# First attention group of a fused cross-attention and FFN kernel: source's order on SyncE and TensorE, bulk loads placed behind the turned probabilities, and a different number of value steps passed to the next group

## The chip, the cores and the metric

One core of a Trainium2 chip runs the whole program. The metric is device time in microseconds (us), the median over repeated runs; smaller is better. A core has five engines with queues of their own: TensorE (PE in the profile) multiplies matrices, VectorE (DVE) and ScalarE (ACT) work elementwise and move results out of PE's accumulators (PSUM), GpSimd (POOL) works elementwise on SBUF, and SyncE (SP) here only issues DMA transfers. Each engine takes its instructions in the order in which the built program lists them, and an instruction that has to wait holds up all behind it on that engine.

## The reference

Everything is float32. Eight sequences of 128 tokens, width 512, 32 heads of size 128, and an FFN of inner width 1376.

```python
def _L0_xattn_ref(hidden_states, key_value_states, attention_mask, position_bias, ln_weight, w_q, w_k, w_v, w_out):
    x = _rmsnorm(hidden_states, ln_weight)
    h_q = (x @ w_q.T).reshape(b, lq, H, DH)
    h_k = (key_value_states @ w_k.T).reshape(b, lk, H, DH)
    h_v = (key_value_states @ w_v.T).reshape(b, lk, H, DH)
    score = jnp.einsum('bqhd,bkhd->bhqk', h_q, h_k)
    score = score + position_bias[None]
    score = jnp.where(m, score, -jnp.inf)
    score = jax.nn.softmax(score, axis=-1)
    score = jnp.where(m, score, 0.0)
    attn = jnp.einsum('bhqk,bkhd->bqhd', score, h_v).reshape(b, lq, H * DH)
    return hidden_states + attn @ w_out.T
...
x = x + _L0_xattn_ref(_layernorm(x, axis=-1), ctx_4096, mask_BxSxS2_bk0, ...)
x = x + _L0_ffn_ref(_layernorm(x, axis=-1), ...)
```

## The kernel before

The 32 heads are worked on in eight groups of four (g = 0 to 7), and within a group the eight sequences are eight blocks (b = 0 to 7). The program runs through these stages: keys and values of group 0 (k0, v0); queries of all groups, stored to DRAM (`queries`) and loaded back two blocks at a time; the attention of group 0 to 7; the output projection; the FFN. The matrix products are split by Strassen's scheme: seven products of quarters in place of eight, and most of those seven are split once more (the inner products). So there are many sums of weight quarters on GpSimd and many additions of partial products on VectorE.

One block of attention (`probabilities`, L547) takes four score matmuls (sc, one for each head) into one PSUM bank, an addition of the masked bias s (`masked_bias`, L538, computed on GpSimd) and a maximum on VectorE, four exponentials and a sum on ScalarE, a reciprocal on VectorE and four scalings on ScalarE. Then the probabilities are turned (`transpose_p`, L582, by `turn`, L267): VectorE transposes 32x32 blocks into tt, SyncE stores tt to DRAM (`turned`, four buffers in rotation) and loads it back as pT. The product with the values (`attend`, L596: av, four matmuls, then a copy aT on ScalarE and a store) follows three blocks later: block b's turning is put on a list, and `advance(3)` (L1088) takes the one of block b - 3.

Between the blocks TensorE computes the keys and values of the next groups, as a generator of steps, `later_kv` (L644): for each group its keys and then its values. Group 1's keys are seven full products (`seven`, L336). All the others up to group 6 are two full products (`whole`, mm_k or mm_v), one single inner product (m, on two banks that alternate, seven pieces), and two pairs of inner products that run in steps of 16 short matmuls (i_k, i_v; `inner`, L382). A step's result goes out of its bank by a copy on ScalarE (into the k or v tile) or an addition on VectorE, and the bank is free for the next only then. `due` (L992) says how many units of this fill are to be done when block b of group g is finished; a full product counts 4 units (FULL), a step of an inner pair 4 (PART), a piece of the single one 1 (ONE). `late` (L996) is what each group leaves undone of its values, for the next group's blocks to fill.

Order of the work: the kernel is written against a framework that puts the instructions of each engine in an order of its own, by priorities and a timing estimate. An engine handle that is wrapped in `InOrder` (L52) keeps what is issued through it in the order of the source. At the start of group 0 `tensor`, `kv_tensor`, `vector`, `scalar` and `gpsimd` are so wrapped (L1039 to L1043). L1102 takes `tensor`, `vector` and `scalar` back to the framework's order after block 3, L1104 `kv_tensor` after block 7. DMA issues on SyncE in the attention (the bias `load_bias` L811, the weights `load_kv` L131, the queries `load_queries` L816, and the turning) are in the framework's order. A transfer into a tile also waits until the tile that held its buffer before has been read for the last time.

Of the kernel before, what the change touches and what calls it, by code (L numbers as in the profile page):

```python
# [18 lines left out]
BS = 32  # L19
# [45 lines left out]
def xattn_ffn_kernel(  # L65
# [19 lines left out]
    nc = tc.nc  # L85
# [5 lines left out]
    GH = 4  # L91
# [34 lines left out]
    def load_w(name, src, eng=nc.sync):  # L126
        t = wpool.tile([P, DC, GW], F32, tag="w", name=name)
        eng.dma_start(t, src.rearrange("(c p) n -> p c n", p=P))
        return t

    def load_kv(g):  # L131
        cols = bass.ts(g, GW)
        return load_w(f"wk{g}", wkT[:, cols]), load_w(f"wv{g}", wvT[:, cols])

    def load_q(g):
        return load_w(f"wq{g}", wqT[:, bass.ts(g, GW)], sync)
# [24 lines left out]
    kv_w = {0: (wk0, wv0)}  # L161
    x_in = [acts.tile([P, 2, D], F32, tag="a", name=f"x_{i}") for i in range(B // 2)]
    for b in range(B):
        nc.sync.dma_start(x_in[b // 2][:, b % 2, :], x[b])

    vector, gpsimd, scalar, sync = (
        InOrder(tc, e) for e in (nc.vector, nc.gpsimd, nc.scalar, nc.sync)
    )
# [410 lines left out]
        return s  # L579


    def transpose_p(g, b, p):  # L582
        n = f"{g}_{b}"
        pT = work.tile([P, 4, GH, BS], F32, tag="pT", name=f"pT_{n}", bufs=4)
        turn(
            vector, nc.sync, n, p.rearrange("q h (j r) -> q h j r", r=BS), (pT, slice(None))
        )()
        return pT

# [18 lines left out]
    tensor = kv_tensor = nc.tensor  # L608
    pend = []
# [32 lines left out]
    FULL, PART, ONE, FIRST = 4, 4, 1, 3.8  # L642
# [83 lines left out]
    kv_tensor = InOrder(tc, nc.tensor)  # L726
# [46 lines left out]
    for n, _ in enumerate(first_kv()):  # L773
        if n in moments_at:
            pair[moments_at[n]] = norm1_moments(moments_at[n])
        if n in scales_at:
            b = scales_at[n]
# [6 lines left out]
        if n in turns_at:  # L784
            b = turns_at[n]
# [18 lines left out]
    scalar = nc.scalar  # L804
# [3 lines left out]
    vector.tensor_scalar(rs1, mv1[:, :, 1], 1.0, EPS, ALU.mult, ALU.add)  # L808
    InOrder(tc, nc.scalar).activation(rs1, rs1, AF.Sqrt)

    def load_bias(g):  # L811
        pb = work.tile([P, GH, S], F32, tag="pb", name=f"pb{g}")
        nc.sync.dma_start(pb, pbias[g * GH : (g + 1) * GH].rearrange("h q k -> q h k"))
        return pb

    def load_queries(g, i, eng=nc.sync):  # L816
        q = acts.tile([P, GH, 2 * S], F32, tag="a", name=f"q_{g}_{i}")
        eng.dma_start(q, queries[g][:, :, bass.ts(i, 2 * S)])
        return q
# [5 lines left out]
    v = kvs[0][1]  # L825
# [12 lines left out]
    for g in range(NG):  # L838
# [13 lines left out]
        w, heads, name = rows_now, [], f"q{g}"  # L852
# [44 lines left out]
    biases, ahead = {0: load_bias(0)}, {}  # L897
# [8 lines left out]
    gpsimd, vector, kv_tensor = nc.gpsimd, nc.vector, nc.tensor  # L906
# [85 lines left out]
    def due(g, b):  # L992


        tiles, steps = 2 * (4 * FULL + 7 * ONE), 2 * 7 * PART
        late = 5 * PART  # L996
        if g == 0 and b < 4:
            return (5 + 2.5 * b) * FIRST
        if g < NG - 2:
            start = 12.5 * FIRST if g == 0 else g * (tiles + steps) - late  # L1000
            end, n, k = (g + 1) * (tiles + steps) - late, 4 if g == 0 else B, b - 4 if g == 0 else b
        else:
            start, n, k = g * (tiles + steps) - late, B, b
            end = start + late + 25 * FULL
        return start + (end - start) * (k + 1) / n - 1.5

    todo = [(g, i) for g in range(NG) for i in range(B // 2)]
    for g in range(NG):
        kT, v = kvs.pop(g)
        pb = biases.pop(g)  # L1010
        if g + 1 < NG:
            biases[g + 1] = load_bias(g + 1)
        if g + 2 < NG:
            kv_w[g + 2] = load_kv(g + 2)
        if g == 0:

            ctx_later = Later()
            products = later_kv()
        if g == NG - 2:
            wo_later = Later()  # L1020
            load_wo(2)(wo_later)
        if g == NG - 1:
            tensor, vector = InOrder(tc, nc.tensor), InOrder(tc, nc.vector)
            fetched, next_fetched = {}, {}
            gpsimd, sync, wo_sums = InOrder(tc, nc.gpsimd), InOrder(tc, nc.sync), None
            biased = [masked_bias(gpsimd, g, k, pb) for k in range(2)]

            bulk = InOrder(tc, nc.scalar)
            come[1, 0] = load_att(1, 0, bulk)
        for b in range(B):  # L1030
            if (g, b) == (NG - 2, B - 1):
                come = {(0, 0): load_att(0, 0, nc.sync)}
            if b % 2 == 0:
                qT = ahead.pop((g, b // 2))
                at = todo.index((g, b // 2)) + 2
                if at < len(todo):
                    ahead[todo[at]] = load_queries(*todo[at], nc.sync if g + 1 < NG else bulk)

            if (g, b) == (0, 0):  # L1039
                tensor = kv_tensor = InOrder(tc, nc.tensor)  # L1040
                vector, scalar, gpsimd = (
                    InOrder(tc, e) for e in (nc.vector, nc.scalar, nc.gpsimd)
                )  # L1043
                done = next(products) + next(products)
            if g == NG - 1:


                if b + 2 < B:
                    biased.append(masked_bias(gpsimd, g, b + 2, pb))
                for _ in range(2):  # L1050
                    wo_later.next(gpsimd)
                if wo_sums:
                    wo_sums = wo_sums(gpsimd)

                def between():
                    if b == 0:
                        next(products)
                    fetched[b] = att_sums(b, 0, come.pop((b, 0)), vector)

                p = probabilities(g, b, qT, kT, pb, between, biased.pop(0))  # L1060
            elif g == 0 and b < 4:
                def one():
                    nonlocal done
                    done += next(products)

                def one_and_sum():
                    ctx_later.next(vector)
                    one()

                if b == 0:  # L1070
                    biased = [masked_bias(gpsimd, g, k, pb) for k in range(2)]
                biased.append(masked_bias(gpsimd, g, b + 2, pb))
                p = probabilities(g, b, qT, kT, pb, one_and_sum, biased.pop(0), one)
            elif g == 0 and b < 6:
                def three_sums():
                    for _ in range(3):
                        ctx_later.next(vector)

                p = probabilities(g, b, qT, kT, pb, three_sums, biased.pop(0))
            else:  # L1080
                p = probabilities(g, b, qT, kT, pb)
                for _ in range(2):
                    ctx_later.next(vector)
                if g == NG - 2:
                    for _ in range((0, 1, 1, 1, 1, 2, 2, 2)[b]):
                        wo_later.next(InOrder(tc, nc.gpsimd))
            pend.append((g, b, transpose_p(g, b, p), v))
            advance(3)  # L1088

            if g == NG - 1:  # L1090
                while next(products, None):
                    pass
            else:
                while done < due(g, b):
                    done += next(products)
            if (g, b) == (NG - 2, 2):

                sums.close()
                wos = pools(outp)("wosA", 2, side="right", reuse_waits="tile")
                load_wo(0)(wo_later)  # L1100
                load_wo(1)(wo_later)
            if (g, b) == (0, 3):  # L1102
                tensor, vector, scalar = nc.tensor, nc.vector, nc.scalar
            if (g, b) == (0, B - 1):  # L1104
                kv_tensor = nc.tensor
            if (g, b) == (1, B - 1):
                gpsimd = nc.gpsimd
            if g == NG - 1:
                if b == 0:
                    proj.close()  # L1110
                    wos = pools(outp)("wosB", 2, reuse_waits="tile")

                    first_banks = [
                        pl.tile([P, 2, HW], F32, tag=tag, name=f"m{k}_0")
                        for k, (pl, tag) in enumerate(2 * [(ps_mm, "mm")] + 2 * [(ps_b, "i")])
                    ]
                    first_out = out_products(0, list(range(NG)), first_banks, fetched)
                n = (b + 2) % B, (b + 2) // B
                come[n] = load_att(*n, bulk)
                if b < NG - 3:  # L1120
                    wo_sums = load_wo(b + 3)
                if b:
                    next(first_out)
                if b + 2 >= B:
                    next_fetched[n[0]] = att_sums(*n, come.pop(n), gpsimd)


    scalar = InOrder(tc, nc.scalar)
# [15 lines left out]
    vector, gpsimd = nc.vector, nc.gpsimd  # L1144
# [78 lines left out]
    scalar = nc.scalar  # L1223
    for i in range(1, B // 2):
# [10 lines left out]
        tensor = nc.tensor  # L1235
# [105 lines left out]
    vector, t3 = InOrder(tc, nc.vector), h2[0, 1]  # L1341
# [227 lines left out]
    for b in range(HB):  # L1569
# [5 lines left out]
        sa, vector = coming[0], nc.vector  # L1575
# [43 lines left out]
```

## Time and profile before

| what | value |
|---|---|
| median of 3 runs | 1056.53 us (1056.42 to 1056.57) |
| the profiled execution, its own time | 1060.24 us |
| its span, first to last instruction | 1058.4 us |
| queries of all groups end, group 0's attention begins | about 227 us |
| score matmuls of group 0, blocks 0 to 7 | 230.7, 237.0, 243.1, 247.4, 254.6, 260.8, 266.0, 270.0 us |
| av matmuls of group 0, blocks 0 to 4 | 251.7, 256.4, 261.7, 266.9, 274.3 us |
| a block of scores or an av, start to start | 0.89 us |
| a full fill product, start to start | 1.73 us |
| mean granted TensorE clock | 0.998 |

The page of the profile gives the busy time of each engine, the chain of work that ended last, and the costliest groups of instructions. Other views list who waited for whom, the instructions of one engine in order of time, and the busy time in chosen windows. In a timeline line the columns are start, duration, engine, source line, operation, output and inputs, shapes and count; in square brackets stands idle time before it and what ended that. L60 is the line of the `InOrder` helper, so all wrapped instructions carry it. Names of tiles are shown without their numbers.

### The profile page before, as it was taken

To read this page: it belongs to the slowest core of one execution; us is meant where nothing else is said; L and a number is where in the kernel's file an instruction comes from. 1 tells how busy PE (TensorE), PEld (TensorE's weight loads), DVE (VectorE), ACT (ScalarE), POOL (GpSimd) and SP (SyncE) were. 2 spreads that over 40 slices of the span, in tenths; PEclk is the share of its full clock that TensorE was granted. 3 is DMA by queue.
4 is the path that set the end of the run, shared out by engine and by line. 5 is a ranking of instruction groups with operands and counts; after the bars stand their busy time and mean duration, and the time that the engine had idled before them with its cause. 6 is when DMAs were issued, how large, how long until landed. Compare 5 with 4: busy or idle time off the path is not lost.

```text
span 1058.4 us, 15313 instructions
## 1 busy us (share of the span) xinstructions
PE 1048.6 (99%) x5288; PEld 859.0 (81%) x5288; DVE 723.0 (68%) x1407; ACT 380.7 (36%) x1146; POOL 558.6 (53%) x647
## 2 busy tenths in 40 slices
PE   9999999999899999999999999999999999999998
PEld 5658888876789898988889779998888865667887
DVE  4698888885577777777777645664544247889852
ACT  2541112027555656556555555531000012333100
POOL 6649776808657666656662275570000336997010
PEclk9999999999999999999999999999999999999999
DMA  8443453495555654655656567773442622120011
GB/s 283 149 170 139 155 184 120 147 359 194 176 177 179 191 184 157 208 179 182 199 170 206 179 217 233 237 277 120 164 139 67 196 99 60 41 60 0 1 40 41
DMA packets 125854, 166.11 MB, mean 157 GB/s; under 512 B 15728, under 2 KB 77424, under 8 KB 125776
## 3 DMA queue, kind: packets, MB, share of 16 engines
q1 hardware_dynamic: 111360, 133.92, 38.5%
q10 hardware_dynamic: 12544, 24.38, 6.6%
q0 software_dynamic: 1872, 6.82, 2.1%
q8 instruction: 42, 0.69, 0.3%
q14 instruction: 36, 0.29, 0.1%
HBM read 106.90 MB, written 58.20 MB: 156 GB/s over the span
## 4 chain that ended last, share of the span: by engine, by line
PE 93%; DMA 3%; POOL 2%; DVE 1%; ACT 1%; issue 1%; SPq 0%; ACTq 0%; DVEq 0%; POOLq 0%
PE i_q L60 9%; PE m L967 9%; PE m L60 8%; PE i_v L437 7%; PE d L1525 6%; PE i L1390 6%; PE i_k L404 6%; PE mm_v L522 6%; PE mm_k L501 6%; PE mm_f L1430 5%; PE mm_q L60 4%; PE av L600 4%; PE sc L555 4%; PE mm_k L60 2%; PE mm_v L60 2%; PE m_v L437 2%
## 5 line engine op out<-in xcount | busy, mean ns | idle before, releaser
L60 DVE TENSOR_TENSOR q<-q,i_q 128x512 f32<-128x512 f32 x168 | 94.6, 596 | 20.2 <-PE i_q L60 17.7
L568 ACT ACTIVATE s<-s,nmx 128x128 f32<-128x128 f32 x240 | 93.3, 390 | 28.2 <-DVE nmx L563 20.7
L399 DVE TENSOR_TENSOR v<-v,i_v 128x256 f32<-128x256 f32 (+1 forms) x150 | 76.5, 521 | 33.6 <-PE i_v L437 29.2
L540 POOL TENSOR_TENSOR s<-pb,mneg 128x512 f32<-128x512 f32 x40 | 61.4, 1536 | 66.0 <-DVE tt L272 66.0
L578 ACT ACTIVATE s<-s,ri 128x128 f32<-128x128 f32 x240 | 76.7, 390 | 43.3 <-DVE ri L576 32.1
L399 DVE TENSOR_TENSOR k<-k,i_k 128x512 f32<-128x512 f32 (+1 forms) x105 | 59.3, 587 | 26.2 <-PE i_k L404 25.9
L605 ACT COPY aT<-av 128x512 f32<-128x512 f32 x60 | 35.1, 586 | 114.2 <-PE av L600 98.9
L60 POOL TENSOR_TENSOR s<-pb,mneg 128x512 f32<-128x512 f32 x24 | 36.7, 1535 | 52.7 <-DVE tt L60 36.0
L555 PEld LDWEIGHTS sc<-k,q 128*128 128x128 f32 x416 | 53.9, 192 | 7.0 <-issue 5.3
L555 PE MATMUL sc<-k,q 128*128 128x128 f32 x416 | 55.6, 275 | 0.0
L1164 POOL TENSOR_TENSOR x<-x,u 128x256 f32<-128x256 f32 x4 | 3.0, 754 | 90.9 <-DVE x L1163 90.9
L60 PE MATMUL m<-wo,a 128*128 128x256 f32 x200 | 48.5, 380 | 0.5 <-DMA a<-att 0.5
L967 PE MATMUL m<-wo,a 128*128 128x256 f32 x200 | 48.4, 379 | 0.0
L272 DVE STREAM_TRANSPOSE tt<-s 128x512 f32<-128x512 f32 x52 | 36.8, 709 | 16.3 <-ACT s L578 15.9
L300 DVE TENSOR_TENSOR S_a<-a 128x256 f32<-128x256 f32 x22 | 10.1, 461 | 54.9 <-DMA a<-att 33.3
L600 PE MATMUL av<-pT,v 128*128 128x128 f32 x360 | 47.6, 275 | 0.0
L568 ACT ACTIVATION_READ_ACCUMULATOR s<-s,nmx 128x1 f32 x240 | 44.9, 187 | 0.0
L559 DVE TENSOR_TENSOR s<-sc,s 128x512 f32<-128x512 f32 x52 | 35.3, 679 | 12.5 <-PE sc L555 12.4
L600 PEld LDWEIGHTS av<-pT,v 128*128 128x128 f32 x360 | 43.8, 192 | 0.0
L967 PEld LDWEIGHTS m<-wo,a 128*128 128x128 f32 x200 | 38.0, 190 | 5.2
L60 PEld LDWEIGHTS m<-wo,a 128*128 128x128 f32 x200 | 37.2, 190 | 5.5 <-DMA a<-att 0.9
L60 DVE TENSOR_TENSOR gate<-gate,i 128x512 f32<-128x512 f32 (+1 forms) x60 | 32.9, 592 | 5.3 <-PE i L1390 4.6
(489 smaller groups left out, 2824.9 us busy)
## 6 DMA issues: line engine op xcount, KB each, us to landing
queries<-q SPq DMA_DIRECT2D x32, 512.0 KB, 3.8
turned<-tt SPq DMA_DIRECT2D x64, 256.0 KB, 2.8
pT<-turned SPq DMA_DIRECT2D x64, 256.0 KB, 3.1
att<-aT ACTq DMA_DIRECT2D x64, 256.0 KB, 3.0
q<-queries SPq DMA_DIRECT2D x30, 512.0 KB, 5.1
a<-att SPq DMA_DIRECT2D x23, 512.0 KB, 4.1
wq<-in_wqT_dram SPq DMA_DIRECT2D x8, 1024.0 KB, 6.6
wk<-in_wkT_dram SPq DMA_DIRECT2D x7, 1024.0 KB, 6.1
```

The source lines that it names most:

```text
L60: return self.tc.keep_in_program_order(getattr(self.engine, op)(*args, **kw))
L399: vector.tensor_tensor(to, *(base or [to]), out, ADD)
L404: kv_tensor.matmul(out, a[n][i], b[n][i], start=first, stop=True, skip_group_check=True)
L437: kv_tensor.matmul(out[:, bass.ts(k, S)], b[n][i][:, bass.ts(k, S)], a[n][i], start=first and k == 0, stop=True, skip_group_check=True,)
L501: kv_tensor.matmul(out, w[i][:, c, bass.ts(t, P)], src[i][:, c, :], start=(first and c == 0), stop=(c == HC - 1), skip_group_check=True,)
L522: kv_tensor.matmul(out[:, bass.ts(k, HW)], src[i][:, c, bass.ts(2 * t + k, S)], w[i][:, c, :], start=(first and k == 0 and c == 0), stop=( ...
L555: tensor.matmul(sc[:, j, :], qT[:, j, bass.ts(b % 2, S)], kT[j][:, cols], start=True, stop=True)
L568: scalar.activation(s[:, j, :], s[:, j, :], AF.Exp, bias=nmx[:, j : j + 1], accum_out=sm[:, j : j + 1],)
L578: scalar.mul(s[:, j, :], s[:, j, :], ri[:, j : j + 1])
L600: tensor.matmul(av[:, j, :], v[b // 2][:, b % 2, bass.ts(j, P)], pT[:, :, j, :], start=True, stop=True,)
L967: tensor.matmul(m[n], sa[n][:, c, :], wo_t[g][n][:, c, :], start=(g == order[0] and c == 0 and PRODUCTS.index(n) % 2 == 0), stop=(g == ord ...
L1390: nc.tensor.matmul(out, a[n][k], fine_t[n][k], start=first, stop=True, skip_group_check=True)
```

## The change

- `load_kv` can load keys' or values' weights alone and takes the queue's handle. In group 0 only wk2 is loaded at the start, through an in-order handle; wv2 is issued after block 5's turning.
- The turning in group 0 issues its store and its load back through an in-order SyncE handle (`turn_sync`); in the other groups as before.
- The bias of the next group is issued through an in-order handle in all groups.
- In group 0 the queries that were loaded at the start of each even block are loaded after that block's turning, in order.
- `tensor` stays in source's order through block 7 of group 0, not only to block 3.
- `late` is 2 steps of 4 units, not 5.

```diff
-    def load_kv(g):
+    def load_kv(g, kinds="kv", eng=nc.sync):
         cols = bass.ts(g, GW)
-        return load_w(f"wk{g}", wkT[:, cols]), load_w(f"wv{g}", wvT[:, cols])
+        return [load_w(f"w{k}{g}", {"k": wkT, "v": wvT}[k][:, cols], eng) for k in kinds]
...
-    def transpose_p(g, b, p):
+    def transpose_p(g, b, p, sync):
...
-            vector, nc.sync, n, p.rearrange("q h (j r) -> q h j r", r=BS), (pT, slice(None))
+            vector, sync, n, p.rearrange("q h (j r) -> q h j r", r=BS), (pT, slice(None))
...
-    def load_bias(g):
+    def load_bias(g, eng=nc.sync):
...
-        late = 5 * PART
+        late = 2 * PART
...
+        turn_sync = nc.sync if g else InOrder(tc, nc.sync)
         if g + 1 < NG:
-            biases[g + 1] = load_bias(g + 1)
+            biases[g + 1] = load_bias(g + 1, InOrder(tc, nc.sync))
         if g + 2 < NG:
-            kv_w[g + 2] = load_kv(g + 2)
+            kv_w[g + 2] = load_kv(g + 2, "kv" if g else "k", turn_sync)
...
-                if at < len(todo):
+                if g and at < len(todo):
...
-            pend.append((g, b, transpose_p(g, b, p), v))
+            pend.append((g, b, transpose_p(g, b, p, turn_sync), v))
+            if g == 0 and b % 2 == 0:
+                ahead[todo[b // 2 + 2]] = load_queries(*todo[b // 2 + 2], turn_sync)
+            if (g, b) == (0, 5):
+                kv_w[2] += load_kv(2, "v", turn_sync)
             advance(3)
...
             if (g, b) == (0, 3):
-                tensor, vector, scalar = nc.tensor, nc.vector, nc.scalar
+                vector, scalar = nc.vector, nc.scalar
             if (g, b) == (0, B - 1):
-                kv_tensor = nc.tensor
+                tensor = kv_tensor = nc.tensor
```

More of the change, by code (lines that the diff above doesn't have):

```diff
@@ L809, in xattn_ffn_kernel @@
     InOrder(tc, nc.scalar).activation(rs1, rs1, AF.Sqrt)
-    def load_bias(g):
+    def load_bias(g, eng=nc.sync):
         pb = work.tile([P, GH, S], F32, tag="pb", name=f"pb{g}")
-        nc.sync.dma_start(pb, pbias[g * GH : (g + 1) * GH].rearrange("h q k -> q h k"))
+        eng.dma_start(pb, pbias[g * GH : (g + 1) * GH].rearrange("h q k -> q h k"))
         return pb
```

## The prediction

> **What bounds the kernel now.** The page comes first. TensorE is busy for 1048.6 of 1058.4 us, and the chain that ended last runs through it.
>
> ```profile
> PE 1048.6 (99%) x5288; PEld 859.0 (81%) x5288; DVE 723.0 (68%) x1407; ACT 380.7 (36%) x1146; POOL 558.6 (53%) x647
> PE 93%; DMA 3%; POOL 2%; DVE 1%; ACT 1%; issue 1%; SPq 0%; ACTq 0%; DVEq 0%; POOLq 0%
> ```
>
> So this change, which removes no matmul, can win only TensorE's idle time and what follows from it. The list of TensorE's waits says where that is, and the windows around the first group of attention say what clock was granted there.
>
> ```profile
> PE av L600 <- DMA pT<-turned: 4.1, 2, 3.3
> ...
> 250.00:260.00 10.00, 9.21 (x42) 5.92 (x41) 7.01 (x12) 5.71 (x22) 8.96 (x14) 1.00 0.67 230
> 260.00:270.00 10.00, 10.00 (x65) 9.28 (x64) 4.23 (x8) 8.39 (x30) 9.26 (x7) 1.00 0.36 121
> 270.00:280.00 10.00, 6.72 (x46) 6.56 (x45) 4.14 (x9) 5.03 (x21) 0.78 (x3) 0.83 0.82 266
> ```
>
> The waits' columns are total us, times, longest. The windows' are length, busy time of PE, PEld, DVE, ACT and POOL, granted clock, DMA share, GB/s. Two products of turned probabilities with values (av) waited for their operand's load, 0.79 and 3.28 us, and the 3.28 us gap was followed by matmuls at less than full clock (0.83 over ten us; every other window that I read shows 1.00). The timelines of TensorE and of SyncE's queue show both places.
>
> ```profile
> 254.56 1.05 PE L555 MATMUL sc<-k,q 128*128 128x128 f32 x8
> 256.40 1.13 PE L600 MATMUL av<-pT,v_back 128*128 128x128 f32 x8 [0.79 <-DMA pT<-turned]
> ...
> 270.00 1.06 PE L555 MATMUL sc<-k,q 128*128 128x128 f32 x8
> 274.35 0.91 PE L600 MATMUL av<-pT,v_back 128*128 128x128 f32 x6 [3.28 <-DMA pT<-turned]
> ...
> 247.62 0.39 SPq L128 DMA_DIRECT2D wv<-in_wvT_dram  x1
> 248.74 0.37 SPq L279 DMA_DIRECT2D pT<-turned  x1
> 250.76 0.33 SPq L274 DMA_DIRECT2D turned<-tt  x1
> 256.92 0.36 SPq L279 DMA_DIRECT2D pT<-turned  x1
> ...
> 264.03 0.33 SPq L274 DMA_DIRECT2D turned<-tt  x1
> 267.96 0.37 SPq L813 DMA_DIRECT2D pb<-in_pbias_dram  x1
> 268.44 0.45 SPq L279 DMA_DIRECT2D pT<-turned  x1
> 268.98 0.52 SPq L818 DMA_DIRECT2D q<-queries  x1
> ```
>
> The load of block 1's probabilities (248.74) stands behind 1 MB of weights (247.62) and lands only at 256.4. The load of block 4's stands behind a bias load (267.96) that waits for its buffer, then shares the engines with two query loads, and lands at 274.3.
>
> **Part 1, SyncE in source's order.** Removed from these two places: wv2 goes behind the load of block 5, q_1_0 behind block 4's, pb2 behind block 7's, and the other query loads each behind an even block's. Block 1: its transpose ends at 244.8 as now; its store then meets one 512 KB query load instead of two and the weights; with the median store-to-landing of the page (2.8 and 3.1 us) plus the 1 us that the store of block 1 shows above it now, it lands by 252, and its product is due at 255.45 (scores started 254.56, 0.89 from start to start). Block 4: transposed by 262.7, landed by 269, and due at about 280 in the new order of TensorE, since the fill described below comes first. Both waits go. Lost start to start: 256.40 - 255.45 = 0.95, and 274.35 - (270.00 + 0.89) = 3.46. The slow clock after the gap: 1 - 0.83 of 10 us = 1.7 us, which the mean granted clock of the whole run, 0.998 over 1058.4 us, bears out within its rounding. Sum: 6.1 us won. The loads that go back are wanted later: q_0_2 is issued at 242.5 (now 231.3), needs 6.3 us (median of this stretch) and is wanted at 254.6; wv2 is issued near 274 and its first sum on GpSimd stands behind the twelve sums of k2 and two masked biases, so after 284. These I cost at nothing, under the fill that TensorE runs meanwhile.
>
> **Part 2, two steps and not five.** Three more steps of 16 matmuls, 1.79 us each, run before group 1 begins, and three fewer in group 6. TensorE's total is unchanged: 0. In groups 1 to 6 the built order shows the pattern of before moved by nearly one block (12 units of fill, 12.75 to a block), without back-to-back products on one bank; before had no idle TensorE there, so 0. From the scores of block 1 of group 7 to the end, no compute engine's order differs.
>
> **Part 3, TensorE in source's order through group 0.** This adds waits, and the order of the built program shows two. (a) Now a block of scores and a product stand between the two first-value fills (mm_v1_0, then scores 5, av 2, mm_v1_1). In the new order both fills come first, then scores 5 and av 2, and then at once mm_v1_0 from S_v1, which needs ScalarE's copy of the bank into v1_0. ScalarE's order now puts that copy behind three of the four exponentials of block 5; before, it stood ahead of block 4's scaling. Block 5's exponentials hang on its own scores. The rows of block 5 now:
>
> ```profile
> 260.81 1.05 PE L555 MATMUL sc<-k,q 128*128 128x128 f32 x8
> ...
> 261.97 0.69 DVE L559 TENSOR_TENSOR s<-sc,s 128x512 f32<-128x512 f32 x1 [1.21 <-PE sc L555]
> ...
> 263.42 0.40 ACT L568 ACTIVATE s<-s,nmx 128x128 f32<-128x128 f32 x1
> ...
> 264.58 0.39 ACT L568 ACTIVATE s<-s,nmx 128x128 f32<-128x128 f32 x1
> ...
> 265.30 0.57 ACT L375 COPY v<-mm_v 128x512 f32<-128x512 f32 x1
> ```
>
> Scores to add 1.16, add to first exponential 1.45, three exponentials 264.58 - 263.42 = 1.16, the copy 0.59: 4.36 us after the scores' start. TensorE gets there after scores and av, 2 x 0.89 = 1.78. It stands for 4.36 - 1.78 = 2.6 us, and everything on TensorE behind it with it, as it is in order. From below 2.4 (a copy shows 0.48 from start to start), from above 3.3, if block 4's transpose (0.70) stands before the add. I take 2.6.
> (b) The seven single products of v1 (4 matmuls, 0.45 start to start, 0.61 to the end) alternate on two banks, and each must be added by VectorE (0.42) before the bank is used again. Now score matmuls are spread among them; in source's order the last six follow one another. On one bank back to back: 0.61 + 0.42 + some 0.1 between engines - 0.45 = 0.7 us of waiting, which is the last pair's; three others, one product apart, wait some 0.2 each, and block 6's add and maximum (0.69 each) are in the same queue: 1.2 us. From below 0.7 (the last pair alone), from above 2.0 (three pairs at 0.7).
>
> **Sum.** 6.1 - 2.6 - 1.2 = 2.3 us won. Against the profiled execution: 1060.24 us around a span of 1058.4, so 1057.9. The timed runs are 3.7 us shorter than the profiled one, 1056.53; nothing ties that difference to this stretch, so the same 2.3 us comes off: 1054.3 us.
>
> **The clock after the new gap.** The row: a gap of 3.28 us cost 1.7 us of clock, one of 0.79 nothing. The new gap is about 2.5 us of idle, between them. The bounds: 0 and 1.7, all or nothing as far as the rows show. The only gap that is seen to pay is a third longer, and nothing shorter is; I take 0 for the sum, and keep 1.7 as a rival at half the chance, since by length the new gap is nearer to the one that paid. [...]
>
> **The rivals.**
> 1. As summed, but the new gap costs clock as the old one did: 1054.3 + 1.7 = 1056.0. For it: 2.5 us is nearer to 3.28 than to 0.79. [...]
> 2. The new waits are hidden (a copy slipped between, additions in time): 1056.53 - 6.1 = 1050.4, or some 1052 if one of them is. For it: DVE is busy for only 4.23 of the ten us from 260. Against: engines run in order, and the copy's place is fixed.
> 3. The other side: the stall moves to block 6. wv2, 1 MB, now stands directly ahead of block 6's store. In the rows above a store right behind wv2 took 6.2 us (250.76 to 256.92), and the longest landing of a probabilities' load is 8.5 us. Stored at 278, landed at worst at 292.7, wanted at about 294. If block 5's chain slips more than 1.3 us past that worst case, the product of block 6 waits. It turns the sign when that wait, clock included, passes 2.3 us; at the price of today's stall (3.46 + 1.7) it gives 1054.3 + 5.1 = 1059.4. Against: the usual landing is 3.1 us, which leaves 7 us.
> That the change does not do what it says I exclude for order, since the built program shows the loads behind; rival 3 is what is left of it.
>
> **How the numbers follow.** As summed 0.43, with its bounds (waits of 2.4 + 0.7 to 3.3 + 2.0) 1053.5 to 1055.7; rival 1 0.21; rival 2 0.12; rival 3 0.24. A change below 0.2% (2.1 us) is about what a measurement of this kernel can't tell from none: faster is below 1054.4, slower above 1058.6. Faster: 0.27 of the first case and rival 2, 0.39. Slower: rival 3 but for its milder part, 0.20. Within: 0.41. The range reaches to rival 2 with one wait hidden and just beyond rival 3's price: 1052.0 to 1059.5. The likeliest one's own range is 1053.5 to 1055.7.
>
> **What will show it.** In TensorE's waits the line av from pT should be gone; in its place mm_v L60 waiting for ACT's copy into v near 263, 2.5 us, and m_v waiting for DVE, about 1 us in several pieces. The clock of that window says which of the first two cases it was. In SyncE's timeline wv comes after block 5's load, and pb after block 7's. The prediction is wrong if mm_v does not wait, if an av still does, or if TensorE idles anywhere after 310 us where it did not.

## The result, and the profile after

| | before | after |
|---|---|---|
| median, 7 runs each side by side | 1056.53 us (1056.34 to 1058.93) | 1059.84 us (1059.23 to 1062.98) |
| the profiled execution | 1060.24 us | 1059.23 us |
| its span | 1058.4 us | 1057.3 us |
| mean granted clock of the 7 runs of after | | 1.0 in four, 0.998 in three |

The ratio is 1.0034, 95% interval 1.0022 to 1.0047: 0.34% slower, with the whole interval above 1, and 0.3 us above the predicted range. The first two rows contradict each other: by the profiled executions the change wins 1.0 us, by the medians it loses 3.3. That is the first thing to explain.

The page's busy times of the changed kernel, over the whole span, and TensorE's waits between 240 and 320 us (us in total, times, longest):

```profile
PE 1047.3 (99%) x5288; PEld 857.6 (81%) x5288; DVE 724.9 (69%) x1407; ACT 382.9 (36%) x1146; POOL 558.4 (53%) x647
...
PE mm_v L60 <- ACT v L375: 2.5, 1, 2.5
PE m_v L60 <- DVE v L399: 0.7, 2, 0.5
PE av L60 <- ACT aT L60: 0.5, 1, 0.5
```

No av waits for pT any more. mm_v waits for ScalarE's copy (2.54 us, 2.6 forecast) and m_v for VectorE (0.72 us, 1.2 forecast), as the prediction's Part 3 had them. The third line was not foreseen. The timelines of TensorE, ScalarE and SyncE at that place, and the windows that hold it (length, busy PE, PEld, DVE, ACT, POOL, clock, DMA share, GB/s):

```profile
262.31 1.05 PE L60 MATMUL sc<-k,q 128*128 128x128 f32 x8
263.20 1.06 PE L60 MATMUL av<-pT,v_back 128*128 128x128 f32 x8
266.80 3.69 PE L60 MATMUL mm_v<-S_v,ctx_sb 128*128 128x256 f32 x16 [2.54 <-ACT v L375]
...
264.92 0.40 ACT L568 ACTIVATE s<-s,nmx 128x128 f32<-128x128 f32 x1
...
265.70 0.39 ACT L568 ACTIVATE s<-s,nmx 128x128 f32<-128x128 f32 x1
...
266.09 1.04 ACT L375 COPY v<-mm_v 128x512 f32<-128x512 f32 x2
...
264.69 0.36 SPq L60 DMA_DIRECT2D pT<-turned  x1
...
260.00:270.00 10.00, 7.46 (x43) 6.65 (x42) 2.45 (x5) 6.27 (x21) 7.89 (x6) 1.00 0.48 157
270.00:280.00 10.00, 9.22 (x76) 8.63 (x75) 6.93 (x16) 4.92 (x17) 4.74 (x9) 1.00 0.53 187
```

The bank of mm_v was full before 262.31, yet ScalarE copies it out at 266.09, after three exponentials of a block whose scores were computed at 262.31. Block 4's load is issued at 264.69 and not at 268.44, with no bias load in front. After 277 us TensorE has no idle time over 0.15 us until 738 us, so the groups behind are untouched, as predicted.

### The profile page after: what moved, and what is told of

Same layout as the page of the kernel before. It is cut to its first block, busy times and chain, and to the rows that moved or that the text cites. A ratio compares the mean times of both kernels' runs of the same rounds, so it can differ in the third digit from the quotient of the medians.

```text
span 1057.3 us, 15326 instructions
## 1 busy us (share of the span) xinstructions
PE 1047.3 (99%) x5288; PEld 857.6 (81%) x5288; DVE 724.9 (69%) x1407; ACT 382.9 (36%) x1146; POOL 558.4 (53%) x647
## 4 chain that ended last, share of the span: by engine, by line
PE 94%; DMA 2%; DVE 2%; ACT 1%; issue 1%; ACTq 0%; POOL 0%; SPq 0%; DVEq 0%; POOLq 0%
PE i_q L60 9%; PE m L967 9%; PE m L60 8%; PE i_v L437 7%; PE d L1530 6%; PE i L1395 6%; PE i_k L404 6%; PE mm_v L522 6%; PE mm_k L501 5%; PE mm_f L1435 5%; PE mm_q L60 4%; PE av L600 4%; PE sc L555 4%; PE mm_k L60 3%; PE mm_v L60 2%; PE m_v L437 2%
## 5 line engine op out<-in xcount | busy, mean ns | idle before, releaser
L555 PEld LDWEIGHTS sc<-k,q 128*128 128x128 f32 x384 | 49.7, 192 | 6.5 <-issue 5.0
L555 PE MATMUL sc<-k,q 128*128 128x128 f32 x384 | 51.1, 275 | 0.0
```

The costliest lines, as they stand in the source:

```text
L555: tensor.matmul(sc[:, j, :], qT[:, j, bass.ts(b % 2, S)], kT[j][:, cols], start=True, stop=True)
```

## The experiments

Each was timed in five rounds beside the kernel before on the same chip. There the kernel before has medians of 1057.0 to 1057.3 us, so compare with that, not with 1056.53.

### Both kernels once more

> The kernel before, unchanged, once more. Theory A (the profiled execution of before was not a usual one: its 3.28 us wait of the product of block 4 and the half clock behind it are absent or much shorter in the usual runs, so that Part 1 had at most 6.1 - 3.7 = 2.4 us to win): the timed median is 1056.5 +- 0.4 with spans near 1054.6 and clock 1.0; a profiled execution near 1056.5 shows the wait of av for pT at under 1.6 us in all and no slow clock between 270 and 280 us; one near 1060 shows them again. Theory B (profiling itself costs this kernel 3.7 us, and the stall is in every run): the profiled execution takes about 1060 again while the median is 1056.5, and the wait is again 3 to 3.5 us with 0.83 of the clock.

Measured: 1057.30 us (12 runs, 1056.44 to 1058.56), ratio 0.9995 (0.9987 to 1.0004). The profiled execution took 1057.12. Its waits, TensorE at block 4, SyncE's issue of block 4's load, and the window:

```profile
PE av L600 <- DMA pT<-turned: 2.4, 2, 1.8
...
269.89 1.06 PE L555 MATMUL sc<-k,q 128*128 128x128 f32 x8
272.75 0.91 PE L600 MATMUL av<-pT,v_back 128*128 128x128 f32 x6 [1.81 <-DMA pT<-turned]
...
268.55 0.45 SPq L279 DMA_DIRECT2D pT<-turned  x1
...
270.00:280.00 10.00, 8.19 (x68) 7.55 (x67) 6.85 (x16) 6.95 (x29) 3.80 (x7) 1.00 0.86 273
```

Theory A holds in kind: the usual execution has the shorter wait and no slow clock. Its numbers were too low, since 2.38 us of waits remain (under 1.6 expected) and the median is 1057.3 (1056.5 expected). The load was issued at 268.55 against 268.44 in the first profile, but the product that waited for it started 1.6 us sooner, and the clock stayed at 1.00. Of the 3.12 us between the two profiled executions of one kernel, 1.69 is stall (4.07 against 2.38) and 1.71 the clock, less 0.3 elsewhere. Eleven of these twelve runs are at 0.999 or 1.0, and of the 103 runs of before that were timed beside the kernels below 92 are; the others are at 0.998. So the first profile showed an execution of a kind that is about one in ten.

> The changed kernel, unchanged, once more beside the others. 1059.8 +- 0.8; mm_v waits 2.4 to 2.7 us for ACT in every profile (a wait fixed by the order of instructions, not by when a load lands), the slow clock in some executions only (0.998 instead of 1.0).

Measured: 1060.82 us (8 runs, 1059.05 to 1061.64), ratio 1.0027 (1.0017 to 1.0037). mm_v waits 2.54 us again, to the hundredth: this wait comes from an order of instructions. Five runs have clock 0.998 and take 1060.67 to 1061.64; the three at 1.0 take 1059.05 to 1060.06. In the profiled one, at 0.998, the records show half the clock for one stretch of 3.41 us right behind the wait: 1.7 us lost.

### The eight combinations of the three parts

Diffs against the changed kernel. Without Part 3:

```diff
-                vector, scalar = nc.vector, nc.scalar
+                tensor, vector, scalar = nc.tensor, nc.vector, nc.scalar
             if (g, b) == (0, B - 1):
-                tensor = kv_tensor = nc.tensor
+                kv_tensor = nc.tensor
```

Without Part 2:

```diff
-        late = 2 * PART
+        late = 5 * PART
```

Part 1 alone has both of these edits. The three without Part 1 are the kernel before with the one edit, the other, or both turned round.

Parts 1 and 2: 

> The changed kernel with TensorE's order undone (Parts 1 and 2 stay). Theory A: the two new waits, 2.54 us of mm_v and 0.72 us of m_v, are gone and nothing comes in their place: 1059.84 - 3.3 = 1056.5, between 1055.5 and 1057.0, no gap over 1 us between 250 and 280 us. Rival C (the loss comes from the moved loads or from the two late steps): it stays at 1059 to 1060.5. The prediction's own sum, if the stall of before were in every run, would give 1056.53 - 6.1 = 1050.4.

Parts 1 and 3: 

> The changed kernel with the five late steps put back (Parts 1 and 3 stay). Theory A: the late steps are worth nothing, 1059.8 +- 0.6, mm_v waits about 2.5 us again. Rival D (the two steps bring the loss): 1057 or less.

Part 1 alone: 

> Part 1 alone (SyncE in source's order; five late steps, TensorE's order left to the planner). ScalarE's order has the copy behind block 5's exponentials again. Theory F: TensorE waits over 1.5 us in all for ACT or DVE in 260 to 290 us, 1058.5 to 1062. Theory A without F (Part 1 only wins): as the two moved loads, 1055.4.

Part 3 alone: 

> The kernel before with Part 3 alone (TensorE in source's order through the first group). ScalarE's copy of the first mm_v bank still stands ahead of the exponentials there. Theory F (the new wait comes from ScalarE's order, which the planner drew anew because Part 1 moved the loads, and not from TensorE's order): no wait of mm_v, 1057.3 +- 0.6. The prediction's pricing of Part 3 by itself (2.6 + 1.2): 1061.

Part 2 alone: 

> The kernel before with Part 2 alone. The prediction: 0, so 1057.2 +- 0.5. Theory J (the planner redraws TensorE's and ScalarE's order with it, as it does with Part 1): 1058.5 or more, with a wait of TensorE over 1.5 us between 255 and 300 us that before does not have. The changed kernels with two late steps spend 0.41 us more after the last matmul than those with five: that should be here as well.

Parts 2 and 3: 

> The kernel before with Parts 2 and 3 and without Part 1, the last of the eight combinations. ScalarE has the first copy of the v1 banks ahead of the scaling of block 4 here, as in every kernel without Part 1. Theory F (Part 1 is what puts the copy behind the exponentials): mm_v does not wait, block 4's product does not wait for its load (as with Part 2 alone), only m_v waits for VectorE, about 0.7 us: 1055.7 + 0.7 = 1056.4, between 1055.5 and 1057.2. Theory K (TensorE's order by itself brings the loss, as Part 3 alone suggests at 1061): 1059 or more, with a wait of TensorE over 2 us.

Measured, with what each one's profiled execution shows: TensorE's gaps over 0.15 us between 240 and 310 us, the time lost to half clock (half of each slow stretch), and the rest, which is the execution's time less both.

| parts | median us | ratio (95%) | profiled us | gaps | clock | rest |
|---|---|---|---|---|---|---|
| none | 1057.30 | 0.9995 (0.9987 to 1.0004) | 1057.12 | 2.38 | 0 | 1054.7 |
| 1 | 1067.29 | 1.0091 (1.0078 to 1.0104) | 1068.04 | 7.10 | 5.12 | 1055.8 |
| 2 | 1055.68 | 0.9985 (0.9973 to 0.9996) | 1055.63 | 0.47 | 0 | 1055.2 |
| 3 | 1060.99 | 1.0039 (1.0025 to 1.0054) | 1062.92 | 4.61 | 1.71 | 1056.6 |
| 1, 2 | 1062.50 | 1.0045 (1.0032 to 1.0058) | 1062.44 | 4.85 | 1.71 | 1055.9 |
| 1, 3 | 1064.40 | 1.0064 (1.0051 to 1.0077) | 1064.58 | 5.62 | 3.41 | 1055.5 |
| 2, 3 | 1056.88 | 0.9996 (0.9985 to 1.0007) | 1059.32 | 2.19 | 0 | 1057.1 |
| 1, 2, 3 | 1060.82 | 1.0027 (1.0017 to 1.0037) | 1060.97 | 3.72 | 1.71 | 1055.5 |

The times spread over 12 us and the rests over 2.4: gaps in this one stretch and the clock behind them are most of it. The two rests that stand out, of 3 and of 2, 3, lie in part elsewhere: between 690 and 725 us these two executions lose 1.3 and 1.8 us, and they alone of all the profiles have idle TensorE there. Both are also slower than their medians, by 1.9 and 2.4 us. The parts do not add. Against the runs of before beside them, 1, 2 and 3 by themselves are worth +10.1, -1.4 and +3.8 us; their sum would be +12.5, the whole change has +3.7. Misses: taking Part 3 out did not win 3.3 us but lost 1.5 (+5.2 and not +3.7), beyond even rival C's range. Part 2, priced at nothing, wins by itself and takes 4.9 us off Part 1; with the five late steps back, the changed kernel has +7.1, which neither theory A nor rival D expected, and m_v there waits another 2.51 us for ScalarE's copies. Part 1 alone is 5 us worse than the upper end of theory F. Part 3 alone has no wait of mm_v, as theory F says, yet takes 1061.0, the number that the prediction's price gives, for other reasons (below). Parts 2 and 3 come out as theory F says, but in the profiled execution block 1's product waits 1.45 us for its load, which theory F did not have.

Why Part 2 wins can be seen in its TensorE and its SyncE:

```profile
272.43 0.61 PE L600 MATMUL av<-pT,v_back 128*128 128x128 f32 x4
...
268.42 0.46 SPq L279 DMA_DIRECT2D pT<-turned  x1
```

Block 4's product waits for nothing there: its load is issued as before, and more of the fill stands ahead of the product.

Why taking Part 3 out loses can be followed in the profile of Parts 1 and 2. Its waits, then VectorE's line and GpSimd's:

```profile
PE i_v L60 <- DVE v L399: 3.4, 1, 3.4
...
284.54 0.69 DVE L559 TENSOR_TENSOR s<-sc,s 128x512 f32<-128x512 f32 x1 [5.43 <-POOL s L60]
...
275.48 0.46 POOL L60 TENSOR_TENSOR s_k<-wk 128x128 f32<-128x128 f32 x1 [7.45 <-PE m_v L60]
```

Left to the planner, TensorE runs the scores of the next group's first block early (from 272.94, behind those of block 7); VectorE's addition to them stands in its queue in front of the additions that free i_v's banks, and waits 5.43 us for a masked bias that GpSimd makes only after its sums of k2, which had stood 7.45 us for a product. So Part 3 mends something that Part 1 breaks, and the loss of Part 3 alone is another one: there m_v waits 1.1 us for ScalarE, and block 5's product 3.0 us for its load, which SyncE issues only at 276.19, when the store (269.68) has landed; two query loads stand beside that store (269.06, 270.45).

All four kernels with Part 1 have ScalarE's copy v1_0 behind three or four of block 5's exponentials, and none of the other four has: there it stands ahead of block 4's scaling. The built order of before and after around it, in words:

```
before:  ri 4, copy v1_0, scale block 4, copy aT 2, 4 exponentials of block 5
after:   ri 4, scale block 4, copy aT 2, 3 exponentials of block 5, copy v1_0, copy v1_1
```

### Is it the copy's place in its queue?

> The changed kernel, but ScalarE keeps source's order through block 5 of the first group and not only through block 3, so that the copy of the first mm_v bank stands ahead of block 5's exponentials. Theory A: the 2.54 us wait shrinks to under 0.5 us, all else stays: 1059.84 - 2.3 = 1057.5, between 1056.8 and 1058.0. Rival E (the wait is a place only; something else, such as block 5's chain, is late by as much): the wait moves to another product and the time stays within 0.6 us of 1059.8.

```diff
-                vector, scalar = nc.vector, nc.scalar
+                vector = nc.vector
+            if (g, b) == (0, 5):
+                scalar = nc.scalar
```

Measured: 1060.87 us, ratio 1.0030 (1.0021 to 1.0039). mm_v no longer waits, but m_v waits 2.36 us for the next pair of copies, which source's order has behind block 5's scaling and the copy of a product. Theory A's time is missed. As rival E has it, the wait moves to another product and the loss stays (+3.6 us against the runs of before beside it), but by the theory's mechanism: the same queue, one place further.

> The changed kernel with the four copies of the first values' banks (v1) on VectorE in place of ScalarE; every other instruction keeps its place. VectorE has the first of them behind block 5's maximum, which ended about 1.2 us before ScalarE's third exponential did. Theory H (the loss is the place of the copy in the evicting engine's queue): mm_v waits 0.8 to 1.5 us and not 2.54, the slow clock goes, 1057.3 to 1058.3. Rival E (block 5's chain or TensorE is late for another reason): a wait of 2 us or more stays somewhere in 260 to 285 us, 1059 or more.

```diff
-                    scalar.copy(part(r, c, t), m[t])
+                    (vector.tensor_copy if name == "v1" else scalar.copy)(part(r, c, t), m[t])
```

Measured: 1057.86 us (11 runs, 1057.31 to 1058.32, all at clock 1.0), ratio 1.0004 (0.9995 to 1.0013). Four copies on another engine, every other instruction in place: +0.8 us against before where the changed kernel has +3.3 and +3.7, so 2.5 to 2.9 us back, in the expected range.

```profile
PE mm_v L60 <- DVE v L375: 1.4, 1, 1.4
PE m_v L60 <- DVE v L399: 0.7, 2, 0.5
```

The wait fell from 2.54 to 1.37 us, and the slow clock went with it.

> As the one before, and VectorE keeps source's order through block 4 of the first group, so that the first two copies stand ahead of block 5's addition. Theory H: no wait of mm_v over 0.3 us, no slow clock; 1059.1 (the changed kernel at full clock) - 2.5 = 1056.6, between 1056.0 and 1057.4; the pieces of m_v for VectorE (0.7 us) stay. Rival E: the 2.5 us wait appears elsewhere, 1059 or more.

```diff
-                vector, scalar = nc.vector, nc.scalar
+                scalar = nc.scalar
+            if (g, b) == (0, 4):
+                vector = nc.vector
```

A miss: 1063.24 us, ratio 1.0054 (1.0038 to 1.0070).

```profile
PE mm_v L60 <- DVE k L60: 4.0, 1, 4.0
```

In source's order VectorE adds k1_1 only behind block 4's transpose (263.49, which waits for ScalarE's scaling). The bank of the second mm_v is free after that addition: 4.04 us instead of 2.54. That is theory H's mechanism at another instruction: the bank comes free late because of a place in a queue. Both times a whole queue was held in order to move the copy, and both times the next late instruction set a wait (2.36 and 4.04 us).

### What of Part 1 wins, and what loses

> The kernel before with two loads moved on SyncE's queue and nothing else: pb2 behind the load of block 7's probabilities, wv2 behind that of block 1's; the order of the four compute engines is that of before, instruction for instruction. Theory A (Part 1 had only the usual stall to win): of 0.57 + 1.81 us that av waits for pT in a usual run, the second goes, the first shrinks to the 0.47 us for ScalarE's copy that every changed kernel shows: 1057.3 - 1.9 = 1055.4, between 1054.8 and 1056.0. Rival G (the loads are late for the traffic on the DMA engines and not for the queue): the waits stay, 1056.9 or more.

```diff
-            biases[g + 1] = load_bias(g + 1)
+            biases[g + 1] = load_bias(g + 1, InOrder(tc, nc.sync) if g == 1 else nc.sync)
...
-            kv_w[g + 2] = load_kv(g + 2)
+            kv_w[g + 2] = load_kv(g + 2, "kv" if g else "k")
...
+            if (g, b) == (0, 1):
+                kv_w[2] += load_kv(2, "v", InOrder(tc, nc.sync))
```

Measured: 1055.60 us, ratio 0.9987 (0.9978 to 0.9995). The only gap left in the stretch is 0.47 us for ScalarE's copy. So the two moved loads do what Part 1 was priced for, and 1.9 us of gaps is what there was to win.

> The changed kernel with one piece of Part 1 undone: the first group's query loads go back to where the planner puts them; weights, bias, stores and loads of the probabilities stay in source's order, Parts 2 and 3 stay. The built order of the four compute engines is then that of Parts 2 and 3 without Part 1, ScalarE's copy ahead of block 4's scaling. Theory L (of all that Part 1 moves it is the query loads that redraw the other engines' order and bring the loss): mm_v does not wait, the slow clock goes, m_v keeps its 0.7 us: 1056.4, between 1055.5 and 1057.2. Rival M (the loss is in the transfers themselves, weights behind block 5's load among them): 1059 or more.

```diff
-                if g and at < len(todo):
+                if at < len(todo):
...
-            if g == 0 and b % 2 == 0:
-                ahead[todo[b // 2 + 2]] = load_queries(*todo[b // 2 + 2], turn_sync)
```

Measured: 1056.72 us (11 runs, 1056.22 to 1057.20), ratio 0.9993 (0.9984 to 1.0002). mm_v does not wait; m_v keeps its 0.7 us. Putting back the query loads alone takes 4 us off the changed kernel (-0.3 and not +3.7 against before): theory L. TensorE's waits between 240 and 320 us are then these:

```profile
PE m_v L60 <- DVE v L399: 0.7, 2, 0.5
PE av L60 <- ACT aT L60: 0.5, 1, 0.5
```

> As the one before, and TensorE's order left to the planner (Part 3 undone as well): the order of the compute engines is that of Part 2 alone, with the weights and the bias behind the probabilities. Theory L: no wait over 0.5 us between 250 and 300 us, 1055.6 +- 0.6, as Part 2 alone and as the two moved loads alone. Rival M: 1058 or more.

The diff is that one and the one without Part 3. Measured: 1054.61 us (9 runs, 1054.17 to 1055.15), ratio 0.9976 (0.9967 to 0.9986), the fastest kernel of the study, and 0.4 us below theory L's range. Part 2 alone has the same order on the compute engines and is 1.0 us slower against its own runs of before (-1.4 and not -2.4), while the two profiled executions differ by 0.5; where the rest comes from was not found. The windows:

```profile
260.00:270.00 10.00, 10.00 (x66) 9.28 (x65) 3.62 (x8) 7.39 (x25) 8.02 (x7) 1.00 0.49 159
270.00:280.00 10.00, 10.00 (x80) 9.03 (x78) 8.35 (x20) 7.29 (x28) 6.85 (x12) 1.00 0.70 247
```

TensorE is busy in all of both. What it costs to keep Part 3 is the difference between these two kernels, 2.1 us by the medians. The profiled executions differ by 1.3: 0.75 in waits (1.22 against 0.47) and 0.4 after the last matmul are the largest pieces.

## Why the prediction was wrong, step by step

- **The step that failed: "Sum: 6.1 us won", with "nothing ties that difference to this stretch".** The 3.7 us between the profiled execution and the median were tied to it: a longer landing and the slow clock were the profiled execution's own. In the execution profiled next, which is near its median, the two waits are 0.57 + 1.81 = 2.38 us and cost no clock. Of these the change could win 1.9, and the two moved loads by themselves gave about that (1.6 us in the medians, 1057.15 - 1055.60). The term was three times too large, and it set the sign: 1.9 - 2.6 - 1.2 is a loss of 1.9 us and not a win of 2.3.
- **Block 1, 0.95 us.** Its product was said to be due 0.89 us after the scores. It cannot start then: there is one av bank, and ScalarE's copy of the product before holds it 0.47 us longer, in every kernel where the load is early. Won here: 0.1 us.
- **Part 3's cost, 2.6 + 1.2 us: the size of the first right, the source wrong.** Measured 2.54 and 0.72. The 0.72 takes Parts 2 and 3 together (0.74 with these two alone); with one of them left out no m_v waits for VectorE. The 2.54 takes Parts 1 and 3: of the eight combinations the two with both have it (2.54, 2.64), and the others have no wait of mm_v. Parts 2 and 3 alone have TensorE in source's order and no such wait. What Part 1 adds is the query loads, moved on SyncE, through the place that the planner then gives ScalarE's copy; the prediction costed these later loads at nothing. With these loads and without Part 3 the kernel loses more, in other waits (4.85 us of gaps). The order of the built program was read correctly for what it does, and credited to Part 3 alone.
- **Part 2, costed at 0.** Alone it wins 1.4 us: with more of the fill in front, block 4's product comes at 272.43, where before it was TensorE's turn at 271.06, and its load, issued at 268.42 as before, is there. A step with no matmul added or removed still moved a product past its operand's landing.
- **The clock after the new gap, kept as a rival at half the chance.** That is 0.21 against 0.43, one in three; 8 of 15 runs of the changed kernel are at 0.998. The prediction should have carried half of 1.7 us, and this is one reason why the median is 1059.84 once and 1060.82 the other time.
- **Rival 3, the slower side,** is not what happened: block 6's product waits for nothing. The loss has the sum's own terms, with the gain put right. In the profiled executions at full clock: -2.38 + 3.73 = +1.35 us of gaps, 0.42 more after the last matmul's end (3.68 against 3.26), and 0.3 spread thin: 2.1 (1059.23 - 1057.12). The clock adds 1.7 in about half of the runs. Together 2.1 to 3.8, and the medians say 3.3 and 3.7.
- **No idle TensorE after 310 us where there was none:** held.
- **A slip in the sum:** 1056.53 - 2.3 is 1054.2 and not 1054.3; nothing hangs on it.

What stays open: why the planner answers later query loads with a later copy was not tried. The 0.42 us at the end is in the changed kernel and in three of its variants, and not in others with the same late steps (3.26 and 3.25 in the two with the copies on VectorE, 3.45 with Part 2 alone), so my expectation that it goes with Part 2 was wrong; no run ties it to a part.

## What to carry to other kernels

Before a stall of one profiled execution is booked as a gain, compare that execution with the median of the runs: where it is slower, its stalls and its slow clock are the first suspects for the difference, and the gain is what the median leaves of them. Where a framework plans the queues, an edit on one queue can redraw the order of the others; compare the built orders edit by edit, not only for the whole change, and put each wait down to the edit that brings it. In this chain of in-order queues a wait shrank when its one instruction moved (2.54 to 1.37 us) and went when one kind of transfer did (the query loads); holding a whole queue in order moved it on (2.36 and 4.04 us).

## What the runs showed of the hardware

A gap of TensorE was followed by a lower clock in some executions of a kernel and not in others. By the longest gap of the profiled execution and the mean granted clocks of the runs: with 1.37 us none of 11 runs is below 1.0, with 1.81 (set by a landing; 3.28 in the execution profiled first) one of 12 is at 0.998, with 2.36 eight of 10, with 2.54 eight of 15, with 3.38 five of 6 (0.996 or 0.998), with 4.04 all of 5 (0.997 or 0.998). In the first profile of before the records show half the clock for 3.41 us, in that of Part 1 alone for twice that.

Where the half clock stands against the gap differs too. Two stretches of the first profile of before, one of the changed kernel's, and one of Part 1 alone:

```profile
272.01:275.42 3.41, 1.07 (x9) 1.11 (x10) 0.57 (x1) 2.79 (x12) 0.00 (x0) 1.00 0.99 334
275.42:278.83 3.41, 3.41 (x19) 3.41 (x17) 1.86 (x4) 0.78 (x2) 0.00 (x0) 0.50 0.45 143
...
265.16:268.57 3.41, 1.77 (x8) 1.62 (x9) 0.18 (x1) 2.67 (x11) 2.81 (x2) 1.00 0.76 247
...
274.85:278.26 3.41, 1.38 (x11) 1.03 (x9) 1.02 (x3) 3.13 (x14) 0.00 (x0) 1.00 1.01 360
```

In the first TensorE is idle for 2.34 us of its gap of 3.28; the next is at half clock, and begins 1.07 us after the matmuls have gone on (274.35). The third holds 1.64 us of the changed kernel's gap of 2.54 (0.90 lies in the 3.41 us before it), and from there to the last matmul that execution's clock is 1.00. The last has 2.03 us idle of a gap of 2.65; its clock is 1.00, and the four matmuls that end the gap at 279.01 take 1.22 us, where four of them take 0.61 at full clock. The changed kernel's other profile has the same gap of 2.54 us and half clock behind it, so the length of the gap alone does not decide; what does was not shown.

A load of 256 KB issued at the same time (268.44, 268.55) let the product that waited for it start 5.9 or 4.2 us later in two executions of one kernel, with DMA shares of 0.82 and 0.86 in the ten us from 270. The product waited 3.28 us in the one and 1.81 in the other; with Part 2 alone it came 4.0 us behind the issue (268.42, 272.43) and waited for nothing.
